# One over root of the norms' variances: ScalarE root and VectorE reciprocal, or a GpSimd power

## The chip, the cores and the metric

The kernel runs on one core of a Trainium2 chip. The metric is the device time of one execution in microseconds (us), as the median of several runs; lower is better. The core has five engines that run in parallel, each through its own instructions strictly in program order: TensorE (PE in the profile, PEld for its weight loads), VectorE (DVE), ScalarE (ACT), GpSimd (POOL) and SyncE (SP, which here only issues DMAs). They wait for one another by semaphores.

## The reference

Four layers work on an image batch x of shape (4, 56, 56, 128), each as `x = x + layer(_gn(x))`. Layers 0 and 3 are a window attention followed by a full attention over all 3136 pixels and an MLP, layer 1 is a selective scan in four directions, layer 2 is a deformable convolution. What this change concerns is the norms in them, all of which have one over the root of a variance:

```python
def _gn(v, G=32, eps=1e-5):
    g = v.reshape(B_, H_, W_, G, C_ // G)
    m = jnp.mean(g, axis=(1, 2, 4), keepdims=True)
    s = jnp.var(g, axis=(1, 2, 4), keepdims=True)
    return ((g - m) / jnp.sqrt(s + eps)).reshape(v.shape)

# layers 0 and 3, twice each (before the full attention, before the MLP)
def _layernorm(x, g, b, eps=1e-05):
    m = jnp.mean(x, axis=-1, keepdims=True)
    v = jnp.mean((x - m) ** 2, axis=-1, keepdims=True)
    return (x - m) * jax.lax.rsqrt(v + eps) * g + b

# layer 1, at its end
y = (y - mu) * jax.lax.rsqrt(var + LN_EPS) * ln_w + ln_b
```

## The kernel before

The four images are done one after the other, and per image the four layers. x lies in SBUF as 128 channels (partitions) by 3136 pixels, and most loops run over 7 chunks of 448 pixels. All phases below are written with a manual schedule: the order of the calls in the source is the order of the instructions on every engine, and nothing is reordered afterwards.

**Where the change sits.** Two helpers hold it. `group_norm` (line 117) is called 4 times per image, 16 in all: once at the head of each layer. It multiplies statistics by a small matrix on PE into PSUM (`gn_pv`, line 130), takes a root on ACT (line 132) and a reciprocal on DVE (line 133), for a 128x1 tile `gn_rstd`. `ln_spread` (line 150) is called once per chunk of every layer norm: 7 times in each of the 8 window phases, 7 in each of the 8 MLPs and 7 in each of the 4 ends of layer 1, 140 in all. Its PE products (`ln_pv`, line 156) give 448 variances as 112x4; ACT takes the root (line 158), DVE the reciprocal (line 159) into `ln_rs`. Later in program order `ln_rows` (line 167) or `scale` of `mamba_out` (line 1173) spreads `ln_rs` over all partitions again by PE (`ln_pb`).

**Window phase** (lines 376 to 470; windows at 219 to 302). A loop over u runs a pipeline of eight bands of windows together with the layer norm of chunk u-2. For one u the calls are, in this order: `scores(u)`, `out(u-1)`, `some` (four products `pm` on PE and their maxima `mx` on DVE, lines 349 and 350), `tokens(u+2)` (line 222, on POOL), `exponentials(u)` (line 267, ACT), `center(u-2)` (line 147 on PE, 383 on ACT), `normalize(u)` (sum and reciprocal on DVE, lines 271 and 272, then two products `pz` on POOL, line 275), `project(u+1)`, `spread(u-2)` (the helper above), `queries(u+1)`, `values(u+1)`, `some`, `scale(u-2)` (`ln_rows`: PE line 167, a copy on ACT line 168, a product on DVE line 392), `keys(u+1)` (four instructions on ACT, line 241), `some`, `turn(u)` (PE, line 281), `shift(u-2)` (ACT, line 395, writes `oTi`), `turned(u)` (ACT, line 286), `inputs(u-2)` (PE, lines 400 and 406), `some`, `weigh(u)`. Chunk 0 to 6 of the norm thus meets u = 2 to 8, and the band loop ends at u = 7.

At the head of that phase, `attention` clears `ks` and `qs` on POOL (lines 323, 324), then `group_norm` is called, then POOL clears `kl` (377), `xw0` (219), `qp0`, `kb0`, `pz0` (225), `xw1`, `qp1`, `kb1`, `pz1`. The first two bands' tokens are made on DVE (line 222, from x, `gn_mean` and `gn_rstd`); the first DVE instruction of them needs the clearing of `xw0`, which it overwrites.

**MLP** (lines 643 to 710). One chunk ahead: center, two of the four hidden products with GELU on ACT (680), spread, the other two, residual, `ln_rows`, result. **End of layer 1** (`mamba_out`, lines 1139 to 1195): per chunk c spread(c); mean(c+1) (PE 1149, DVE 1153, ACT 1155); gate(c+1) (DVE 137, PE 1163, ACT SiLU 1164); out(c-1) (PE 1184, DVE 1185); scale(c) (PE 1173, DVE 1175, ACT 1177, DVE 1178). POOL has nothing in this loop.

ScalarE's functions need a table: an instruction ACT_TABLE_LOAD stands in ACT's stream wherever the next function is not in the table loaded last. Roots, exponentials (267, 549, 819, 1002), GELU (680), SiLU (791, 1164) and logarithms (827) are of different tables here; copies, squares and identities (with scale and bias) cause none.

Of the kernel before, what the change touches and what calls it, by code (L numbers as in the profile page):

```python
# [10 lines left out]
F32 = mybir.dt.float32  # L11
F32R = mybir.dt.float32r
I32 = mybir.dt.int32
AF = mybir.ActivationFunctionType
ALU = mybir.AluOpType
# [4 lines left out]
P = 128  # L20
# [14 lines left out]
NKB = (L + KB - 1) // KB  # L35
QB = 112
NTB = L // QB
LP = NKB * KB
MW = 512
KW = L // MW * MW  # L40
# [14 lines left out]
def _swin_cols():  # L55
    return [("wq", 128), ("wk", 128), ("wv", 128), ("wo", 128),
            ("w1", 512), ("w2", 512), ("b1", 4), ("bq", 1), ("bk", 1),
            ("bv", 1), ("bo", 1), ("b2", 1), ("g1", 1), ("be1", 1), ("g2", 1), ("be2", 1)]


COLS = {
    "C": [("ident", 128), ("gmat", 128), ("center1", 128), ("center2", 128), ("others2", 128), ("ones1", 1), ("ones2", 1), ("lo", 1), ("dmask", TB), ("halves", HW), ("base", 2 * KK * NTB)],
    "L0": _swin_cols(),
# [7 lines left out]
def _offsets(cols):  # L71
    at, n = {}, 0
    for name, w in cols:
        at[name] = (n, w)
        n += w
    return at, n


class _Net:
    def __init__(self, ctx, tc, x, packs, out):  # L80
        self.tc, self.nc, self.x_in, self.out = tc, tc.nc, x, out
        self.B = x.shape[0]
        nc = self.nc
        wp = ctx.enter_context(tc.tile_pool(name="weights", bufs=1))
        self.keep = wp
        self.w = {}
        for i, (layer, cols) in enumerate(COLS.items()):
            at, n = _offsets(cols)
            t = wp.tile([P, n], F32, tag=f"w_{layer}", name=f"w_{layer}")
            (nc.sync if i % 2 == 0 else nc.scalar).dma_start(t, packs[layer])  # L90
            self.w[layer] = {name: t[:, o : o + k] for name, (o, k) in at.items()}
        c = self.w["C"]
        self.ident, self.gmat = c["ident"], c["gmat"]
        self.ones = {1: c["ones1"], 2: c["ones2"]}
        self.center = {1: (c["center1"],), 2: (c["center2"], c["others2"])}
        self.sel = wp.tile([P, KB], F32R, tag="sel", name="sel")
        nc.vector.memset(self.sel.bitcast(F32), 0.0)
        for h in range(NH):
            nc.vector.memset(self.sel[h * DK : h * DK + 2, :].bitcast(F32), 1.0)
        self.ident2 = wp.tile([64 + NX, NX], F32R, tag="ident2", name="ident2")  # L100
        nc.vector.memset(self.ident2.bitcast(F32), 0.0)
        for k in (0, 64):
            nc.vector.tensor_copy(self.ident2[k : k + NX, :], self.ident[:NX, :NX])
        self.one32 = wp.tile([P, DK], F32, tag="one32", name="one32")
        nc.vector.memset(self.one32, 1.0)
        self.eps = wp.tile([P, 1], F32, tag="eps", name="eps")
        nc.vector.memset(self.eps, 1e-5)
        self.x = wp.tile([P, L], F32, tag="x", name="x")
        self.st = wp.tile([P, NCK, 6], F32, tag="gn_st", name="gn_st")
        self.dpool = ctx.enter_context(tc.tile_pool(name="tables", bufs=1, space=DRAM))  # L110
# [6 lines left out]
    def group_norm(self, sb, ps):  # L117
        nc = self.nc
        st = self.st
        mv = sb.tile([P, 2], F32, tag="gn_mv", name="gn_mv")  # L120
        nc.vector.bn_aggr(mv, st.rearrange("p c s -> p (c s)"))
        pm = ps.tile([P, 512], F32, tag="mm", name="gn_pm")
        nc.tensor.matmul(pm[:, 0:1], lhsT=self.gmat, rhs=mv[:, 0:1], start=True, stop=True)
        mean = sb.tile([P, 1], F32, tag="gn_mean", name="gn_mean")
        nc.vector.tensor_copy(mean, pm[:, 0:1])
        dv = sb.tile([P, 1], F32, tag="gn_dv", name="gn_dv")
        nc.vector.tensor_sub(dv, mv[:, 0:1], mean)
        nc.vector.scalar_tensor_tensor(dv, dv, dv, mv[:, 1:2], ALU.mult, ALU.add)
        pv = ps.tile([P, 512], F32, tag="mm", name="gn_pv")
        nc.tensor.matmul(pv[:, 0:1], lhsT=self.gmat, rhs=dv, start=True, stop=True)  # L130
        rstd = sb.tile([P, 1], F32, tag="gn_rstd", name="gn_rstd")
        nc.scalar.activation(rstd, pv[:, 0:1], AF.Sqrt, bias=self.eps)
        nc.vector.reciprocal(rstd, rstd)
        return mean, rstd

    def gn_apply(self, out, x, gn):
# [13 lines left out]
    def ln_spread(self, sq, bank, sb):  # L150

        nc, n, k = self.nc, sq.shape[1], sq.shape[2] // QB
        pv = bank("ln_pv")
        for i in range(k):
            for j in range(n):
                nc.tensor.matmul(pv[:QB, i : i + 1], lhsT=sq[:, j, i * QB : (i + 1) * QB], rhs=self.ones[n][:, 0:1], start=(j == 0), stop=(j == n - 1))
        rs = sb.tile([QB, k], F32, tag="ln_rs", name="ln_rs")
        nc.scalar.activation(rs, pv[:QB, :k], AF.Sqrt, bias=self.eps[:QB])
        nc.vector.reciprocal(rs, rs)
        return rs  # L160

    def ln_rows(self, dst, rs, bank):
# [144 lines left out]
    def attention(self, layer, x, x1, oT, sb):  # L307
# [9 lines left out]
        nc, tc, w = self.nc, self.tc, self.w[layer]  # L317
        ks = sb.tile([P, LP], F32, tag="ks", name="ks")
        qs = sb.tile([P, LP], F32, tag="qs", name="qs")
        nm = sb.tile([P, L], F32R, tag="nm", name="nm")  # L320
# [892 lines left out]
    def deform(self, b, x):  # L1213
# [4 lines left out]
        tab = self.tables[b]  # L1218
        n2 = NTB * KK
        nq = CH // QB  # L1220
        with tc.tile_pool(name="df", bufs=1) as s1, tc.tile_pool(name="df_ps", bufs=1, space=PSUM) as s1x, tc.manual_schedule():
            idx = s1.tile([QB, n2], I32, tag="idx", name="idx")
            wps = s1x.tile([P, 2, 512], F32, tag="wt", name="wt")
            nw = 4 * KK * NTB // 2
            wts = [wps[:QB, i, :nw].rearrange("q (n k) -> q n k", k=4) for i in range(2)]
            with tc.tile_pool(name="dc", bufs=1) as sb, tc.tile_pool(name="dc_ps", bufs=6, space=PSUM) as ps:
# [4 lines left out]
                xg = sb.tile([P, L], F32, tag="xg", name="xgd")  # L1231
                gt = sb.tile([QB, NTB, P], F32, tag="gt", name="gt")
                tv = tab.rearrange("(t r x) (k c) -> r x t k c", r=2, x=TR, k=4)
# [68 lines left out]
            with tc.tile_pool(name="dg", bufs=2) as sb, tc.tile_pool(name="dg_ps", bufs=2, space=PSUM) as ps:  # L1302
# [10 lines left out]
                def weigh(t):  # L1313
                    g = patch[t].rearrange("q k (s c) -> q (k s) c", s=4)
                    wv = wts[2 * t // NTB][:, t % (NTB // 2) * KK : (t % (NTB // 2) + 1) * KK, :].rearrange("q k s -> q (k s)")
                    for k in range(0, 4 * KK, 12):
# [22 lines left out]

                for t in range(NTB + 1):  # L1340
                    if t < NTB:
# [117 lines left out]
```

## Time and profile before

| | |
|---|---|
| median of 14 runs | 13500.58 us (13492.34 to 13531.18) |
| the profiled execution: its own time | 13510.05 us |
| the profiled execution: span from first to last instruction | 13508.0 us |
| granted TensorE clock, mean | 0.936 |
| busy: DVE, ACT, POOL | 9225.0, 7563.5, 9948.9 us |
| ACT roots: lines 158 and 132 | 140 of 264 ns, 16 of 262 ns |
| DVE reciprocals: lines 159 and 133 | 140 of 178 ns, 16 of 164 ns |
| ACT_TABLE_LOAD, all lines | 365 of 1283 ns |
| a window phase (last image, layer 3) | 12642 to 12812 us |
| an end of layer 1 (last image) | 12136 to 12223 us |
| an MLP (last image, layer 3) | 13429 to 13505 us |

Times inside the span are given as us from its start. A line of the timeline reads: start, duration, engine, source line, operation, output<-inputs, shapes, count, and in brackets how long the engine was idle before it and what ended that idle time. In the chain of waits (the work that ended last, followed back) a line is start, duration, engine, tile, source line. In the groups it is the line, engine, operation, tiles, shapes and count, then busy us and mean ns.

### The profile page before, as it was taken

The numbers are of one execution on the slowest core, as the hardware profiler recorded it, in microseconds if no ns is written. First come the engines' busy times: TensorE is split into PE (matmuls) and PEld (weight loads), VectorE is DVE, ScalarE is ACT, GpSimd is POOL, SyncE is SP. The second block draws the span as 40 slices with busy tenths as digits, with TensorE's granted clock in tenths as the row PEclk, the third lists the DMA queues.
The fourth block names the chain that finished last, engine by engine and source line by source line (L and its number), as shares of the span: only waits on it lengthen the run. The fifth ranks groups of instructions, "written<-read, shape, count | busy, mean of one in ns | idle before, by whom it ended". The sixth has DMA issues, their size and how long they took to land.

```text
span 13508.0 us, 221295 instructions
## 1 busy us (share of the span) xinstructions
PE 11968.5 (89%) x87732; PEld 7700.9 (57%) x87732; DVE 9225.0 (68%) x11159; ACT 7563.5 (56%) x19130; POOL 9948.9 (74%) x6852
## 2 busy tenths in 40 slices
PE   8989995799998999579999899957999989995799
PEld 4448883544544888454454488845445448883544
DVE  6649993464665999446466599945646659993564
ACT  5567761356556776135655677613565567761356
POOL 4949994487494999448759499943975949994397
PEclk9999997899999999789999999978999999997899
DMA  2000004200000000420000000042000000004200
GB/s 98 1 13 5 4 4 123 68 1 8 4 1 13 5 4 4 127 64 1 8 4 1 13 5 5 3 129 63 1 11 1 1 13 5 5 3 132 60 1 6
DMA packets 181186, 344.79 MB, mean 26 GB/s; under 512 B 20104, under 2 KB 101416, under 8 KB 180024
## 3 DMA queue, kind: packets, MB, share of 16 engines
q0 software_dynamic: 80640, 231.28, 6.1%
q1 hardware_dynamic: 99224, 97.83, 2.3%
q8 instruction: 693, 11.35, 0.4%
q14 instruction: 341, 2.79, 0.1%
q10 hardware_dynamic: 288, 1.53, 0.0%
HBM read 256.04 MB, written 74.52 MB: 24 GB/s over the span
## 4 chain that ended last, share of the span: by engine, by line
PE 32%; DVE 9%; issue 3%; POOL 3%; ACT 3%; DMA 0%; SPq 0%; another core or an unknown queue 0%; DVEq 0%; POOLq 0%; ACTq 0%
PE pm L349 7%; DVE hs L1066 6%; PE po L571 4%; PE pst L547 3%; PE pst L542 2%; PE yt L1084 2%; PE dbu L1048 2%; PE pvt L1328 2%; POOL hs L1075 1%; PE pyb L1100 1%; DVE mx L350 1%; POOL g L1308 1%; DVE dgb L952 1%; PE pd L560 1%; PE pss L257 1%
## 5 line engine op out<-in xcount | busy, mean ns | idle before, releaser
L555 POOL TENSOR_TENSOR es<-es,e 128x896 f32<-128x896 f32 x2016 | 4160.9, 2090 | 131.4 <-ACT e L549 73.5
L350 DVE TENSOR_REDUCE mx<-pm 128x1 f32<-128x512 f32 (+1 forms) x4928 | 3058.2, 671 | 1413.3 <-PE pm L349 797.4
L549 ACT ACTIVATE e<-pst 128x448 f32<-128x448 f32 (+1 forms) x5600 | 2678.4, 544 | 1897.4 <-PE pst L547 1349.4
L1066 DVE TENSOR_TENSOR_SCAN hs<-da,dbu 128x928 f32<-128x928 f32 x1792 | 3632.9, 2070 | 54.5 <-ACT dbu L1059 30.3
L1075 POOL TENSOR_TENSOR hs<-hs,cb 128x896 f32<-128x896 f32 x1792 | 3464.0, 1944 | 25.5 <-ACT carry L1070 19.5
L349 PE MATMUL pm<-ks,qs 32*128 32x512 f32 (+1 forms) x9856 | 2917.2, 637 | 13.4 <-DVE nm L371 7.8
L547 PE MATMUL pst<-qs,ks 32*128 32x448 f32 x11200 | 2688.7, 548 | 0.0
L1084 PE MATMUL yt<-w_C,hs 128*116 128x128 f32 x14336 | 1866.0, 273 | 1.2 <-POOL hs L1075 1.2
L542 PE MATMUL pst<-nm,sel 32*128 32x448 f32 x5600 | 1640.0, 615 | 0.0
L1084 PEld LDWEIGHTS yt<-w_C,hs 128*116 128x116 f32 x14336 | 1571.0, 135 | 2.2 <-POOL hs L1075 2.1
L1048 PE MATMUL dbu<-dgb,ut 112*128 112x224 f32 x7168 | 1258.6, 298 | 269.1 <-DVE hs L1066 269.0
L1308 POOL DMA_INDIRECT g<-tab,idx x1008 | 943.5, 936 | 629.8 <-issue 435.5
L571 PE MATMUL po<-e,va 128*32 128x448 f32 (+1 forms) x11200 | 1352.4, 551 | 0.1
L349 PEld LDWEIGHTS pm<-ks,qs 32*128 32x128 f32 x9856 | 924.4, 186 | 746.4 <-DVE mx L350 621.1
L1328 PE MATMUL pvt<-w_C,g 112*128 112x112 f32 x4032 | 665.8, 324 | 701.9 <-issue 590.3
L1048 PEld LDWEIGHTS dbu<-dgb,ut 112*128 112x128 f32 x7168 | 945.3, 192 | 534.6 <-DVE hs L1066 524.5
L1002 ACT ACTIVATE da<-dl,A 128x112 f32<-128x112 f32 x3584 | 1194.5, 383 | 0.1
L547 PEld LDWEIGHTS pst<-qs,ks 32*128 32x128 f32 x11200 | 1099.8, 185 | 103.6 <-issue 14.7
L1328 PEld LDWEIGHTS pvt<-w_C,g 112*128 112x128 f32 x4032 | 561.1, 180 | 815.7 <-issue 792.2
L542 PEld LDWEIGHTS pst<-nm,sel 32*128 32x128 f32 x5600 | 570.6, 184 | 740.5 <-DVE mx L350 387.1
L1329 ACT COPY vt<-pvt 128x336 f32<-128x336 f32 x336 | 142.3, 441 | 1417.0 <-remote 972.3
L1070 ACT COPY carry<-hs 128x32 f32<-128x32 f32 x1792 | 398.1, 222 | 623.0 <-DVE hs L1066 614.9
(228 smaller groups left out, 15355.6 us busy)
## 6 DMA issues: line engine op xcount, KB each, us to landing
tab<-zero SPq DMA_DIRECT2D x4, 6728.0 KB
g<-tab,idx POOLq DMA_INDIRECT x1008
tab<-gt SPq DMA_DIRECT2D x32, 448.0 KB
dl_d<-dl SPq DMA_DIRECT2D x28, 448.0 KB
dl<-dl_d SPq DMA_DIRECT2D x56, 224.0 KB
tab<-gt SPq DMA_DIRECT2D x32, 336.0 KB
out_dram<-x SPq DMA_DIRECT2D x28, 224.0 KB
x<-in_x_dram SPq DMA_DIRECT2D x21, 224.0 KB
```

Of the source, the lines that this page charges most:

```text
L349: nc.tensor.matmul(pm[:, :m], lhsT=qs[head(h), q.start : q.start + P], rhs=ks[head(h), keys], start=True, stop=True)
L350: nc.vector.tensor_reduce(mx[:, home[i][1], h, kc : kc + 1], pm[:, :m], AX.X, ALU.max)
L542: nc.tensor.matmul(t[:, :CH], lhsT=self.sel[head(h), :], rhs=nm[head(h), part(qc)], start=True, stop=False)
L547: nc.tensor.matmul(t[:, :CH], lhsT=ks[head(h), k * KB : (k + 1) * KB], rhs=qs[head(h), part(qc)], start=False, stop=True)
L549: nc.scalar.activation(e[:nk, j, :], t[:nk, :CH], AF.Exp, scale=SCALE)
L555: nc.gpsimd.tensor_tensor(s, es[g - 1, p][:nk] if k == 1 else s, e[:nk], ALU.add)
L571: nc.tensor.matmul(m["po"][head(h), :CH], lhsT=va[:nk, k, head(h)], rhs=src(h)[:nk], start=(k == 0), stop=(k == NKB - 1))
L1048: nc.tensor.matmul(pu[:, 8 * h : 8 * h + 8, 2 + tb * TB : 2 + (tb + 1) * TB], lhsT=made[g]["ut", 2 * r + tb][:, d, :], rhs=made["r", g // ...
L1066: nc.vector.tensor_tensor_scan(flat(pairs[u // 2][:, d % 2]), flat(made[g]["da"][:, r]), flat(banks.pop(u)), 0.0, ALU.mult, ALU.add)
L1075: nc.gpsimd.tensor_tensor(hs, hs, made["r", g // 2]["cb"][:, :, r * HW : (r + 1) * HW], ALU.mult)
L1084: nc.tensor.matmul(sums[q][:YR, e * P : (e + 1) * P], lhsT=hs[:, n, :], rhs=self.ident, start=(n == 0), stop=(n == NST // 2 - 1), is_trans ...
L1328: nc.tensor.matmul(pt[:, m, :], lhsT=g[:, k + m, s * P : (s + 1) * P], rhs=self.ident[:QB, :QB], start=(s == 0), stop=(s == 3), is_transpo ...
```

## The change

The root on ACT becomes an addition of epsilon on DVE (PSUM to SBUF), and the reciprocal on DVE becomes a power of -0.5 on POOL, in place, with a constant tile of exponents as second operand. The constant tile `eps` goes, `half` (128x4) comes.

```diff
+EPS = 1e-5
+NQ = 4
...
-        self.eps = wp.tile([P, 1], F32, tag="eps", name="eps")
-        nc.vector.memset(self.eps, 1e-5)
+        self.half = wp.tile([P, NQ], F32, tag="half", name="half")
+        nc.vector.memset(self.half, -0.5)
...
         rstd = sb.tile([P, 1], F32, tag="gn_rstd", name="gn_rstd")
-        nc.scalar.activation(rstd, pv[:, 0:1], AF.Sqrt, bias=self.eps)
-        nc.vector.reciprocal(rstd, rstd)
+        nc.vector.tensor_scalar_add(rstd, pv[:, 0:1], EPS)
+        nc.gpsimd.tensor_tensor(rstd, rstd, self.half[:, 0:1], ALU.pow)
...
         rs = sb.tile([QB, k], F32, tag="ln_rs", name="ln_rs")
-        nc.scalar.activation(rs, pv[:QB, :k], AF.Sqrt, bias=self.eps[:QB])
-        nc.vector.reciprocal(rs, rs)
+        nc.vector.tensor_scalar_add(rs, pv[:QB, :k], EPS)
+        nc.gpsimd.tensor_tensor(rs, rs, self.half[:QB, :k], ALU.pow)
```

## The prediction

> **What bounds the kernel now.** I read the page's busy times first, then the table loads by source line, then the timeline and the chain of waits of each stage that calls the two helpers.
>
> ```profile
> PE 11968.5 (89%) x87732; PEld 7700.9 (57%) x87732; DVE 9225.0 (68%) x11159; ACT 7563.5 (56%) x19130; POOL 9948.9 (74%) x6852
> ```
>
> Over the span PE is busiest and ACT least, so work taken from ACT pays only where ACT's turn comes last. The change can act in the stages with norms alone: 8 window phases (about 165 us each), 8 MLPs (76), 4 ends of layer 1 (87) and 16 group norms.
>
> ```profile
> L158 ACT ACT_TABLE_LOAD  x132: 1283/1283/1283, 62.0 to 13491.8; - x132
> ```
>
> The root's own price on ACT is small (264 ns); the table loads are what it costs: 132 here, 8 at line 132, and those that bring the other table back. Without roots one load per phase stays: at line 267, 48 become 8, at 680, 56 become 8, at 1164, 28 become 4, at 549, 8 become none. That takes away 132+8+40+48+24+8 = 260 loads, 334 us of ACT, and 41 us of roots. How little of it is on the path, one window iteration (u = 4, layer 3, last image) shows in the timeline:
>
> ```profile
> 12724.10 1.28 ACT L267 ACT_TABLE_LOAD   x1
> 12724.13 2.22 DVE L350 TENSOR_REDUCE mx<-pm 128x1 f32<-128x448 f32 x4 [0.44 <-PE pm L349]
> ...
> 12725.40 0.86 ACT L267 ACTIVATE s<-s 128x784 f32<-128x784 f32 x1
> ...
> 12726.28 0.97 DVE L271 TENSOR_REDUCE m<-s 128x16 f32<-128x784 f32 x1
> 12726.70 1.28 ACT L158 ACT_TABLE_LOAD   x1
> ...
> 12726.74 0.95 PE L156 MATMUL ln_pv<-w_C,ln_sq 128*112 128x1 f32 x8 [0.26 <-ACT ln_sq L383]
> ...
> 12727.69 3.08 POOL L275 TENSOR_TENSOR pz<-s,m 64x784 f32<-64x784 f32 x2 [13.81 <-DVE m L272]
> ...
> 12728.29 0.18 DVE L159 RECIPROCAL ln_rs<-ln_rs 112x4 f32<-112x4 f32 x1 [0.75 <-ACT ln_rs L158]
> ...
> 12729.58 1.14 PE L167 MATMUL ln_pb<-w_C,ln_rs 112*128 112x112 f32 x8
> ...
> 12730.75 0.53 ACT L168 COPY ln_sq<-ln_pb 128x448 f32<-128x448 f32 x1 [1.86 <-PE ln_pb L167]
> ...
> 12731.18 2.37 ACT L241 ACTIVATE kb<-pk,w_L 32x392 f32<-32x392 f32 x4
> ...
> 12733.58 0.76 ACT L395 ACTIVATE oTi<-ln_sq,w_L 128x448 f32<-128x448 f32 x1
> ```
>
> PE waited only 0.26 us for all that both loads and the root delay. The root's result was there at 12728.5, a microsecond before PE got to `ln_pb` at 12729.58. From `ln_pb` on, the chain runs through ACT: copy, four `kb`, `oTi`, and then PE's line 400.
>
> **The price of the power, p.** No row shows a power on POOL. The nearest are its elementwise products:
>
> ```profile
> L994 POOL TENSOR_TENSOR du<-dl,xa 128x112 f32<-128x112 f32 x896 | 408.3, 457 | 1.8 <-DMA dl<-dl_d 1.5
> L1011 POOL TENSOR_TENSOR dh<-du,dh 128x448 fp32r<-128x448 f32 x224 | 255.6, 1141 | 30.4 <-ACT dh L1007 30.4
> ```
>
> From 112 to 448 elements costs 684 ns, 2.0 ns each, so a product of 4 elements would be an estimated 0.24 us. A power has more steps. Lower end 0.15 us (POOL's clearing of 128x64 takes 152 ns), upper end 0.94 us, its dearest non-streaming row (an indirect DMA, 936 ns); I take 0.5, near the 112-element product. A software routine several times dearer is kept as a rival. The addition on DVE I put at 0.16 us, as other 128x1 operations there (line 125), plus 0.05 a hand-over.
>
> **Window phases, the term that decides.** `spread(u-2)` comes after `normalize(u)` in program order, so on POOL the power stands behind the two `pz` (12727.69 to 12730.77), although its input is ready at about 12727.9. Neither starts earlier: `pz` needs lines 271 and 272 on DVE, these stand behind the four `mx`, which end at 12726.35 and come from PE. The earlier exponential (12724.1 instead of 12725.4) therefore frees nothing here; in u = 5, where line 271 had waited 0.39 us for it, it does. So `ln_rs` is ready at 12730.77 + 0.1 + p, and `ln_pb` begins 1.29+p late. The same subtraction gives 1.28 in u = 2, 0.9 in u = 5 and 1.4 in u = 7; I take 1.2+p. Behind `ln_pb` wait PE's next `pm` and `turn`, and on ACT the copy, `kb` and `oTi`, with no gap to absorb it (0.5 us before `oTi` is all, and that follows `kb`). In u = 8 no `pz` stands ahead: nothing. 8 phases x 6 x (1.2+p) = 57.6+48p = **+82 us**.
>
> **Heads of the window phases.** POOL's clearings from `kl` on stood ahead of nothing and ran early; now they queue behind the power, which waits for the statistics. First, DVE's line 222 needs `xw0`: power, `kl` and `xw0` instead of root and reciprocal, +0.54+p (in the three later layer-0 heads less 1.28, a load exposed there). Second, line 222 then meets seven clearings on POOL (8.1 us). What that does, two layer-3 heads show, where one clearing string still ran:
>
> ```profile
> 12645.45 5.63 DVE L222 TENSOR_SCALAR xw<-x,gn_mean,gn_rstd 128x343 f32<-128x343 f32 x3
> ```
>
> ```profile
> 2532.95 1.46 DVE L222 TENSOR_SCALAR xw<-x,gn_mean,gn_rstd 128x343 f32<-128x343 f32 x3
> ```
>
> Undisturbed the three take 0.89 us. In images 0 and 2 DVE got in after one clearing, in 1 and 3 only after the whole string (5236 ns for one instruction). Block per head from 0.7 to 8 us; I take 4.3, half and half. Sum: 8(0.54+p+4.3), less 3x1.28, less the 10.6 us that layer 3's heads lose already: 24+8p = **+28**.
>
> The Trainium skill ("SBUF — State Buffer", Who interferes with whom) has the pair of ports that DVE and GpSimd share held for a whole instruction, with the other engine blocked. The 5.24 us agrees that DVE is shut out, but it lasted over four clearings (1.81 at most), where the rule has it wait for one; by the rule the block would be about 1.8 at most and the sum 20 us lower.
>
> **Other group norms.** Layer 1: the load at line 132 (882.00 to 883.28) and root and reciprocal lay on the path, 1.78 us; now 0.25+p: 4(p-1.53). Layer 2: about 4(p-0.25). Together 8p-7 = **-3**.
>
> **MLPs.** From the second chunk the chain of waits is PE alone, period 9.21 us; root and loads hide behind it. The variance is there at 13454.97, `ln_pb` comes at 13457.17, so the power has some 1.9 us of cover behind one POOL addition long done (13453.99). Uncovered are the first chunk, p-0.24, and 0.2 us that PE waits at 13493.64: 8(p-0.44) = **+0.5**. The GELU's loads leave no gap in PE.
>
> **Ends of layer 1.** Chain of waits:
>
> ```profile
> 12163.85 1.41 ACT xc L1177 x2
> 12165.26 0.02 issue
> 12165.28 1.28 ACT L158
> 12166.58 0.27 ACT ln_rs L158
> 12166.85 0.02 issue
> 12166.87 0.18 DVE ln_rs L159
> 12167.05 1.04 DVE xc L1153 x2
> ```
>
> Here the load is on the path: DVE's reciprocal holds up line 1153 behind it. But next late is DVE itself: line 1178 runs 12165.30 to 12166.39, then the addition, so 1153 starts at about 12166.6 instead of 12167.05. Five chunks x 4 x 0.42 = **-8**. POOL is idle and `ln_pb` comes 8 us later: the power is covered. ACT's SiLU loads lie before a product that PE delivers later. The attention's first load (line 549) is in no chain.
>
> The skill ("ScalarE: Activation LUTs", What ACT_TABLE_LOAD costs) adds 1380 ns of drain to each 1283 ns load. This trace has the root start 0.02 us after its load ended (12727.98, 12728.00). With the drain, layer 1's group norms would gain 5.5 us more.
>
> **Sum:** 57.6+24-7-3.5-8 = 63, and 72p (48+8+8+8): at p = 0.5, +99 us, on the profiled execution's own 13510.05 (span 13508.0). That execution lay 9.5 us above the median of the runs; I carry the difference over to the median, 13500.6+99 = **13600 us**, +0.7%.
>
> **Rivals.**
> 1. *The power is a slow routine.* Nothing in the trace excludes it. Above p = 1.9 the MLPs become bound by it too (8 x 6 chunks, 48 us for each us more): p = 2 gives +212 (13713), p = 4 about +450 (13950).
> 2. *Not slower: the power does not wait for `pz`*, because `pz` gets done, or the power issued, before PE reaches `ln_pb`. The place is POOL's queue in u = 2 to 7, the point from which it decides is `ln_rs` ready by 12729.5. For it: POOL idles 13.8 us ahead of `pz`. Against: the program order, and `mx` ahead of line 271. Then a window phase gains PE's small gaps, 0.26 to 0.8 us in five iterations, 8 x 1.8 = -14, and with the other terms (24-7-3.5-8+24p = +18) the change is +4, or -25 where the heads get in at the first clearing: 13476 to 13535.
> 3. *The loads stay* because other functions still alternate. The ACT list shows only one table besides the root's in each of these phases, so hardly; it would cost +115 or so (no gains in layer 1): 13615.
>
> **Numbers.** Forecast 66%; slow power 18%; not held up 12%; loads stay 4%. The forecast's own range is p 0.15 to 0.94 and heads 0.7 to 8 us: 63+11-29 = +45 to 63+68+30 = +161. For 8 in 10 I reach on to part of rivals 1 and 2: +34 to +220, 13535 to 13720. What a measurement of this kernel can tell from no change is about 0.2%, 27 us. Slower by more: 66+18+4, less 3 = 0.85; within: 0.10; faster: 0.05.
>
> **What would show it.** On POOL's timeline, the power right after the second `pz` in u = 2 to 7 and its duration p; PE idle before `ln_pb`, ended by POOL; window iterations of about 21 us instead of 19.2 to 19.8; heads where line 222 lasts as long as the clearings; 105 table loads left; layer-1 iterations 0.4 us shorter. It is wrong if the power takes several us, or if `ln_pb` isn't late.

## The result and the profile after

The changed kernel takes 13694.01 us (median of 6 runs, 13687.82 to 13702.53) against 13500.58 (28 runs now, 13483.56 to 13531.18): a ratio of 1.0142, 95% interval 1.0132 to 1.0152, **slower by 193 us**. Its profiled execution took 13690.59 us, span 13688.8, granted clock 0.930. The spans of the two profiled executions differ by 180.8 us; the rest lies in where each stood to its median (9.5 above, 3.4 below). In `kernel.py` of the changed kernel, lines behind the two new constants have moved by 2: 158 is 160 (DVE's addition) and 161 (the power), 167 is 169, 222 is 224.

The page's busy times, to set beside the line of before:

```profile
PE 11997.7 (88%) x87732; PEld 7739.2 (57%) x87732; DVE 9267.0 (68%) x11159; ACT 7210.1 (53%) x18713; POOL 10100.3 (74%) x7008
```

ACT lost 353 us (104 table loads are left of 365), POOL gained 151 us (156 powers), and the kernel became slower: neither engine's total was the bound. The powers, in the groups by shape (the figures behind the bar are busy us and mean ns of one, then the idle time ahead and what ended most of it):

```profile
L161 POOL TENSOR_TENSOR ln_rs<-ln_rs,half 112x4 f32<-112x4 f32 x140 | 142.3, 1016 | 508.2 <-DVE ln_rs L160 504.4
L135 POOL TENSOR_TENSOR gn_rstd<-gn_rstd,half 128x1 f32<-128x1 f32 x16 | 9.0, 564 | 71.0 <-DVE gn_rstd L134 71.0
```

So p is 1.02 us for four elements per partition and 0.56 for one. The window iteration that the prediction showed (u = 4, layer 3, last image), in the timeline of after:

```profile
12903.67 0.10 DVE L160 TENSOR_SCALAR ln_rs<-ln_pv 112x4 f32<-112x4 f32 x1
12903.91 3.07 POOL L277 TENSOR_TENSOR pz<-s,m 64x784 f32<-64x784 f32 x2 [16.18 <-DVE ln_rs L160]
12904.35 1.03 PE L351 MATMUL pm<-ks,qs 32*128 32x448 f32 x8
...
12907.06 1.02 POOL L161 TENSOR_TENSOR ln_rs<-ln_rs,half 112x4 f32<-112x4 f32 x1
...
12908.14 1.72 PE L169 MATMUL ln_pb<-w_C,ln_rs 112*128 112x112 f32 x8 [2.76 <-POOL ln_rs L161]
```

The power's input is ready at 12903.77, but POOL starts it 3.3 us later, behind `pz`. PE ends `pm` and stands still for 2.76 us, released by the power; before, the line `ln_pb` had no wait. From the iteration's start (the last `pwy`) to `ln_pb` it is 9.56 us, before 7.25. The eight `ln_pb` products then take 1.72 us; before they took 1.14. At the head of the same phase the chain of waits shows:

```profile
12809.45 0.58 POOL gn_rstd L135
12810.03 0.27 POOL kl L379
12810.30 0.47 POOL xw L221
12810.77 0.03 issue
12810.80 8.62 DVE xw L224 x3
```

Here 8.62 us stand for three DVE instructions that take 0.89 undisturbed, and all eight heads have 8.60. The timeline has DVE's three and POOL's string beside them, the first and the last of the seven clearings shown:

```profile
12810.71 0.73 POOL L227 MEMSET qp<- 128x768 f32 x1
12810.80 8.61 DVE L224 TENSOR_SCALAR xw<-x,gn_mean,gn_rstd 128x343 f32<-128x343 f32 x3 [1.43 <-POOL xw L221]
...
12816.98 1.79 POOL L227 MEMSET pz<- 128x2048 f32 x1
```

Where the 180.8 us lie, from the two traces by stage, all four images together (us, after less before): window phases +191.3, attentions +9.4, MLPs -3.0, heads of layer 1 and its convolution -6.5, scans -1.8, ends of layer 1 -10.3, layer 2 +1.7. Inside the eight window phases: from the group norm to DVE's line 224 +3.9, its first three instructions +51.1 (17.7 to 68.8), from there to the first `pwy` (PE's product of the output weights, one per u, line 299 before) -2.5, the seven iterations from `pwy` to `pwy` +157.8 (997.1 to 1155.0), from the last `pwy` to the attention's first exponential -19.1.

### The profile page after: what moved, and what is told of

Read it like the earlier page. It is cut to its first block, busy times and chain, and to the rows that moved or that the text cites. A ratio compares the mean times of both kernels' runs of the same rounds, so it can differ in the third digit from the quotient of the medians.

```text
span 13688.8 us, 221078 instructions
## 1 busy us (share of the span) xinstructions
PE 11997.7 (88%) x87732; PEld 7739.2 (57%) x87732; DVE 9267.0 (68%) x11159; ACT 7210.1 (53%) x18713; POOL 10100.3 (74%) x7008
## 5 line engine op out<-in xcount | busy, mean ns | idle before, releaser
L277 POOL TENSOR_TENSOR pz<-s,m 64x784 f32<-64x784 f32 x128 | 192.0, 1500 | 832.4 <-DVE ln_rs L160 514.7
```

## The experiments

The theory: (a) in the iterations, POOL's order puts the power behind `pz`; (b) in the heads, the clearings that now run behind the power shut DVE out; (c) TensorE's clock falls to half after the new wait, which the forecast had left out. The rivals are that the power's own price does it all, and that the change acts elsewhere. These runs fell on several chips. On most of them, as `before_again` shows below, the stage of the deformable gathers takes 1312 us instead of 1529, with the other stages alike; so ratios to the kernel before on the same chip are compared, and iterations and heads, which a gather doesn't touch.

**pow_first** issues the power ahead of the products `pz` on POOL:

```diff
 def normalize(t):  # sum and reciprocal on DVE
-    for j in range(2): nc.gpsimd.tensor_tensor(pz...)
+def products(t):
+    for j in range(2): nc.gpsimd.tensor_tensor(pz...)
...
 do("spread", u - 2)
+if u != 1: do("products", u)
```

> The changed kernel, but in the window phases POOL gets the power of spread(u-2) ahead of the two pz products of normalize(u); PE, DVE and ACT keep their order. Theory (the power is late because it stands behind pz on POOL): ln_rs is then ready before PE reaches ln_pb, the window iterations u = 3 to 7 fall from 21.5 to 23.9 us back to 19.2 to 19.9, the seven iterations of all eight phases together from 1155 to about 990 us, and the time from 13694 to about 13530. Rival (the power's own duration of 1.0 us, with the hand-overs DVE to POOL to PE, is what delays): the iterations keep 1 us or more of the loss, time above 13600. Rival (pz itself becomes late, and turn(u) on PE waits for it): PE idle before the pt products instead of before ln_pb, iterations near 21 us.

Measured: 13331.92 us, ratio 1.0049 (1.0032 to 1.0066). The iterations sum to 987.9 us, 9 less than in before; the heads stay at 8.6 us each. In the timeline (u = 5, layer 3, last image):

```profile
12566.76 1.03 POOL L161 TENSOR_TENSOR ln_rs<-ln_rs,half 112x4 f32<-112x4 f32 x1 [12.01 <-DVE ln_rs L160]
...
12567.77 3.07 POOL L281 TENSOR_TENSOR pz<-s,m 64x784 f32<-64x784 f32 x2
...
12568.11 1.14 PE L169 MATMUL ln_pb<-w_C,ln_rs 112*128 112x112 f32 x8
```

The power of the same 1.03 us is done at 12567.79, PE reaches `ln_pb` 0.3 us later without a wait. So the order, not the power's price alone, made the 158 us: (a) holds. The time fell less than expected (about 13530 would be a ratio of 1.0022), and one reason is in the trace: from the last `pwy` to the attention's first exponential it takes 255.5 us again, as in before (254.3), where after has 235.3.

**clear_first** puts the clearings of `kl`, `xw`, `qp`, `kb`, `pz` ahead of the group norm; the power stays behind `pz` (`gn()` is the call of `group_norm`):

```diff
+for t in range(2):
+    for z in (xw, qp, kb, pz): nc.gpsimd.memset(z[t], 0.0)
+gn = gn()
...
-    if t < 2:
-        nc.gpsimd.memset(xw[t], 0.0)
...
-    if t < 2:
-        for z in (qp, kb, pz):
-            nc.gpsimd.memset(z[t], 0.0)
```

> The changed kernel, but kl, xw, qp, kb and pz are cleared on POOL ahead of the group norm's power instead of behind it. Theory (DVE's first token instruction is shut out while the clearings run): the three DVE instructions of line 222 of the kernel before fall from 8.60 us in all eight heads to 0.9 in the layer-0 heads and to 1.5 to 5.7 in the layer-3 heads, as before the change; together with the shorter wait for xw this takes 45 to 55 us off: about 13645. The window iterations stay at 21.5 to 23.9 us. Rival (what delays line 222 is the power or the DVE addition ahead of it, not the clearings): no change, 13694.

Measured: 13437.9 us, ratio 1.0127 (1.0110 to 1.0144), where 13645 would be 1.0107. From the answer on the tile `xw` (ns minimum, median, maximum, then first and last start):

```profile
L226 DVE TENSOR_SCALAR xw<-x,gn_mean,gn_rstd x48: 283/383/509, 23.2 to 12567.9; 128x343 f32<-128x343 f32 x16, 128x28 f32<-128x28 f32 x16, 128x21 f32<-128x21 f32 x16
```

No instruction of the line is over 0.51 us (before 5.24, after 8.21): the three take 0.88 us in every head, so (b) holds. But part of the gain is paid back: in layer 3 the string of clearings (12552.3 to 12561.1 in the last image) is still running when the statistics are there, the power starts at 12561.08 behind it, and from group norm to line 226 it takes 8.17 us in three of the four and 8.40 in the last, instead of 3.56. Heads together 54.3 us against 98.9 in after, iterations unchanged (1167).

**both** has the two edits together.

> pow_first and clear_first in one. Theory (two independent queue effects on POOL carry the loss): the gains add, 13694 - 165 - 50 = about 13480, which is 20 us below the kernel before, from the ends of layer 1 (-10), the group norm of layer 1 (-6) and the last part of the window phases. Rival (the power costs in other places as well): it stays above 13510.

Measured: 13295.21 us (10 runs), ratio 1.0017 (1.0007 to 1.0026); iterations 991.8, heads 53.7. The two losses go away together, but the 20 us below before did not come: the rival's 13510 is a ratio of 1.0007, and the measured one lies above it. Its trace has the attentions 14.1 us longer than `before_again` has, of which more below. `best` and `early` ask what can be won.

**gn_root** gives root and reciprocal (and the constant `eps`) back to the group norms alone, **ln_root** to the row norms alone; the lines are those of gn_root, in ln_root they stand the same for `rs`:

```diff
-nc.vector.tensor_scalar_add(rstd, pv[:, 0:1], EPS)
-nc.gpsimd.tensor_tensor(rstd, rstd, self.half[:, 0:1], ALU.pow)
+nc.scalar.activation(rstd, pv[:, 0:1], AF.Sqrt, bias=self.eps)
+nc.vector.reciprocal(rstd, rstd)
```

> Half of the change: the 16 group norms have root and reciprocal again, the 140 layer norms keep the addition and the power. Theory: the heads of the window phases go back to those before (head and line 222 together minus 55 us), layer 1's group norm gets its table load back (+6), the window iterations stay: about 13645. Rival (heads cost little and the loss is all in the iterations): 13690 or more.

> The complement of gn_root: root and reciprocal for the row norms as in the kernel before, the power on GpSimd for the group norms alone. Theory: the window iterations are those of before (997 us, within 10), all that is lost stays in the heads, where DVE's line 222 is shut out by the clearings as in after (about 8.6 us per head, +50 to +55 us against before), and the group norms of layers 1 and 2 give 5 to 20 us back: ratio 1.002 to 1.004. Rival (heads and iterations act on each other, or the heads' loss is made up within the phase): ratio 1.000 or below, or iterations that differ from before by over 20 us.

Measured: gn_root 13428.33 us, ratio 1.0120 (1.0103 to 1.0137), iterations 1147.4, heads 35.9 (before 43.9). ln_root 13317.69, ratio 1.0039 (1.0023 to 1.0054), iterations 998.9, heads 99.1. Each has one loss whole and the other not at all. The excesses, 1.20% and 0.39%, add up to 1.59%, within the intervals of the 1.48% that the change costs on such a chip (`after_again`).

**mult** (the row norms' power becomes a product in the same place) and **fill** (two matmuls ahead of `ln_pb`) ask how the 157.8 us divide:

```diff
-nc.gpsimd.tensor_tensor(rs, rs, self.half[:QB, :k], ALU.pow)      # mult
+nc.gpsimd.tensor_tensor(rs, rs, self.half[:QB, :k], ALU.mult)
...
 pb = bank("ln_pb")                                                # fill, u = 2 to 7
+for i in range(2):
+    nc.tensor.matmul(pb[:, :CH], lhsT=self.ident, rhs=self.x[:, :CH], start=True, stop=True)
```

> After's kernel with the power of the row norms replaced by a product on the same tiles: the root of the variance is left out, and the instruction stays in its place with its wait. The power's own price: 1.02 us in 112x4 against an estimated 0.24 us for a product of 4 elements. Theory (the power stands on the path in u = 2 to 7, behind pz): ln_pb begins 0.78 us earlier in 48 iterations, -37 us, and with a shorter wait of TensorE (about 1.5 to 2 us instead of 2.3 to 2.8) somewhat less time at half clock, up to -35 us more: iterations 1155 to 1085-1118, ratio 1.009 to 1.0115. pz's 1.2 to 1.3 us stay, so the iterations do not come back to the 997 of before. Rival (the power itself is cheap or hidden, only the order costs): iterations 1150 or more, ratio 1.014.

> After's kernel with two more matmuls of TensorE in each of the window iterations u = 2 to 7 (identity by a 448-column block of x, into the bank of ln_pb, which ln_pb then overwrites), placed ahead of ln_pb, so that TensorE works while it would wait for the power. They add 2.0 us of work per iteration where it waits 2.3 to 2.8. Theory (what the forecast missed in the window iterations, 158 us measured against 48 x (1.2+1.02) = 106, is TensorE's clock falling to half after that wait): TensorE's time at half clock in these iterations goes to nearly none (after: 0 to 10.2 us per iteration), and the seven iterations of the eight phases, 1155 us together, come down by 30 to 55 us, though TensorE has 98 us of work more; the whole about -30 to -60 us against after's 13694, a ratio of 1.010 to 1.012 to the kernel before. Rival (the missing 50 us are waiting of some other kind, and the half clock is only seen with it): the added work cannot help, 1155 us or up to 50 us more, ratio 1.014 or above.

Measured, mult: 13359.47 us, ratio 1.0073 (1.0058 to 1.0088), iterations 1094.7. The product takes 0.20 us:

```profile
L161 POOL TENSOR_TENSOR ln_rs<-ln_rs,half 112x4 f32<-112x4 f32 x140 | 28.1, 201 | 500.4 <-DVE ln_rs L160 496.7
```

Iterations are 60 us below after's, where 0.82 us less in 48 places make 39; the rest goes with the clock (116.0 us of them at half, in after 245.8). The ratio is below the range expected, above all because the MLPs fell too, by 37 us together, which the expectation hadn't priced; TensorE ran 14 us at half clock there, against 94 in after. How the shorter instruction brings that about was not traced.

Measured, fill: 13440.52 us, ratio 1.0131 (1.0116 to 1.0147), iterations 1126.6, 28 to 37 less than in the two traces of the changed kernel though TensorE does more. The ratio misses the range of 1.010 to 1.012, and its interval overlaps that of `after_again`; what shows the effect is the iterations. The window of the iteration u = 4 (last phase), first in after, then in fill (from:to and length, busy us of PE, PEld, DVE, ACT, POOL, then the granted clock):

```profile
12898.00:12920.00 22.00, 19.21 (x140) 12.88 (x139) 13.95 (x27) 9.95 (x20) 6.50 (x6) 0.92 0.00 1
```

```profile
12652.00:12674.00 22.00, 20.11 (x147) 13.16 (x145) 14.34 (x28) 9.92 (x20) 6.50 (x6) 1.00 0.00 1
```

And `ln_pb` in fill, u = 4:

```profile
12658.92 1.77 PE L169 MATMUL ln_pb<-x,w_C 128*128 128x448 f32 x4
...
12661.75 1.15 PE L171 MATMUL ln_pb<-w_C,ln_rs 112*128 112x112 f32 x8 [1.06 <-POOL ln_rs L161]
```

It still waits for the power, but the products behind are back at 1.15 us. TensorE's time at half clock in the 56 iterations: 245.8 us in after, 64.9 in fill, 37.5 in before. With the clock whole the iterations read off the waits themselves:

| iteration, us | u = 4 to 5 | 5 to 6 | 6 to 7 |
|---|---|---|---|
| before | 19.17 | 19.84 | 19.17 |
| mult, typical, clock whole | 20.66 | 20.88 | 20.67 |
| fill, clock whole | 21.48 | 21.71 | 21.48 |
| after, mean of eight | 22.13 | 22.83 | 22.81 |

From before to fill is 2.31, 1.87, 2.31: the forecast's 1.2 + p with p = 1.02. From mult to fill is 0.82: the two prices on POOL, 1.016 less 0.201. From fill to after is 0.65 to 1.33: the clock. After itself confirms it: in the two of its eight phases that have no half clock from u = 4 to 5, that iteration takes 21.49 us, fill's time without fill's matmuls. (c) holds in the iterations, a little below the 30 to 55 us that were expected, since fill keeps 65 us of half clock, most of it behind u = 7. Over u = 2 to 7, fill with the clock whole (20.89, 21.75, 21.48, 21.71, 21.48, 19.78 us) is 14.5 us above before with the clock whole (18.30, 19.45, 19.17, 19.84, 19.17, 16.70): 116 us in eight phases are wait, the other 42 of the 157.8 the clock.

**best** is pow_first with the root kept in the window phases' group norms; **early** is best with `ln_pv` ahead of `pk` on PE and the addition ahead of DVE's sums; **early_root** has early's order with the roots of before. The order of early, against after:

```diff
 do("center", u - 2)
-if u != 1: do("normalize", u)
-do("project", u + 1)
+do("project", u + 1, "q")
 do("spread", u - 2)
+if u != 1: do("normalize", u)
 if u != 1: do("products", u)
+do("project", u + 1, "k")
```

> Both power orders mended in the cheapest way found: in the window phases the power of a row norm goes to GpSimd ahead of the two products pz, and the group norm at the heads of the window phases keeps the root on ScalarE and the reciprocal on DVE; the power stays for the group norms of layers 1 and 2 and for all row norms. From pow_first's ratio of 1.0049 (65 us) less the heads' +55: about +5 us, between -15 and +20, ratio 0.999 to 1.0015; iterations about 990 us, heads (to the end of the first three DVE instructions) about 44 as before, layers 1 and 2 -15 to -25. Rival (the stages' sums decide: iterations -9, heads 0 to -8, layers 1 and 2 -20, nothing lost elsewhere): -30 us, ratio 0.998 or below.

> best, with the row norm's variance taken one place earlier on TensorE (ln_pv ahead of the projection pk instead of behind it) and its addition ahead of DVE's line of sums for pz. In best the power ends at 1.0 us after the point where pz could have begun, so in u = 2 and 3, where no attention group lies between, TensorE waits 1.5 to 1.9 us for pz, and the next stretch often runs 3.41 us at half clock. Theory (the power's 1.0 us ahead of pz is what keeps best at the time of before): power and pz begin about 0.5 to 0.7 us earlier, the waits in u = 2 and 3 fall to about 1 us, iterations 994 to 960-980 us: ratio 0.998 to 0.9995. Rival (the path there runs through ACT's copy, kb and oTi, and pz's wait is hidden behind it): iterations 985 or more, ratio 1.000 to 1.001 as for best.

> The kernel before, with root and reciprocal everywhere, and only the order of early: ln_pv ahead of pk on TensorE, the variance's chain ahead of DVE's line of sums. Theory (early's gain over before needs the loads gone): before's ln_pv already waits 0.26 to 0.80 us for ln_sq, which stands behind the exponential's table load on ACT; without pk ahead of it it waits up to 0.66 us longer, so nothing is gained: iterations 993 to 1020, ratio 0.9995 to 1.002. Rival (early's gain is the order's alone and the power has no part in it): iterations 985 or less, ratio 0.9985 or below.

Measured, best: 13277.91 us (11 runs), ratio 1.0004 (0.9995 to 1.0013): the time of before, not below it. Iterations 994.3. In u = 4 to 6 they are 18.65, 18.78 and 18.65 us, 0.5 to 1.1 below before, but in u = 2 and 3 the power delays `pz` and PE waits for it; one stretch of 3.41 us at half clock then lengthens an iteration from 18.92 to 20.12 us. By stage against `before_again`, layer 1 is 21.3 us shorter, while attentions and MLPs are 24.3 longer, with 118 us at half clock in the MLPs instead of 86.

Measured, early: 13245.51 us (9 runs), ratio **0.9974** (0.9965 to 0.9984), 32 us below before and the one version faster than both kernels. The ratio is below the ranges of both theory and rival, and the mechanism expected was little of it: iterations 990.7, not 960 to 980. Of the 48 us between the traces of best and early, 27 are in the ends of the window phases, 261.9 to 235.1 us together, and 17.5 in the MLPs. For the ends the clock shows why. The windows below begin at the last `pwy` of the last phase, in best, then in early:

```profile
12572.00:12587.00 15.00, 14.10 (x48) 6.93 (x49) 7.43 (x14) 3.36 (x7) 1.01 (x1) 0.54 0.01 2
```

```profile
12530.00:12549.00 19.00, 16.68 (x93) 8.79 (x93) 13.34 (x26) 5.50 (x14) 1.01 (x1) 1.00 0.00 1
```

Ahead of that `pwy` PE waited 0.93 us for `pz` and then 1.84 for `o` (DVE's copy, line 307) in best, 1.15 and 1.84 in early, and behind it PE's order is the same. Yet in best the clock is at half for 13.65 us soon after, in early not at all; the ends hold 184.6 us of half clock in best and 86.6 in early. In each trace all stretches at half clock start on a grid with steps of 3.413 us. In best the wait of 1.84 us lies within one step and is 54% of it; in early an edge of the grid cuts it, and its step is idle for 45%. In seven phases of best the last `pwy` stands at 0.61 to 0.65 of a step, with 21 to 25 us at half clock to follow in the end; in six of early it stands at 0.42 to 0.45, with 10. So what a wait costs depends on where it falls, and early's gain rests partly on that: against `before_again`, 23 us of its gain are these ends and 24 layer 1, and the attentions take 15 back.

Measured, early_root: 13526.24 us (9 runs; 13489.02 before on its chip), ratio 1.0025 (1.0015 to 1.0035). Iterations 1050.3, 0.65 us more in each of u = 4 to 6 as expected, more in u = 2 and 3; both sum and ratio lie above the ranges expected (1020 and 1.002). `ln_pv` waits for the square, which stands behind the exponential and its table load (u = 5):

```profile
12789.85 0.95 PE L156 MATMUL ln_pv<-w_C,ln_sq 128*112 128x1 f32 x8 [1.46 <-ACT ln_sq L383]
```

The new order alone therefore costs time; it needs the loads gone.

**after_again** and **before_again** are the two kernels themselves on one of those chips.

> The changed kernel itself, beside the other runs on one chip. Both theories: about 193 us over before as on the first chip, ratio 1.0142 to 1.0147; window iterations 1155 within 15, first three DVE instructions of the heads 68.8.

> The kernel before itself, for a trace from the same chip as best and early. Window iterations 997, heads 44 us together, and the stage of the deformable gathers as short as in the other runs here (about 1311 instead of 1529 us), with nothing else changed.

Measured: after_again 13477.18 us, ratio 1.0148 (1.0133 to 1.0164), iterations 1163.8, first three DVE instructions 68.8. before_again 13275.03 us, iterations 992.8, heads 35.6 (the two heads that had 5.6 us are not among them here), gathers 1312.1.

## Why the prediction was right, and where its sizes were off

**Direction and place were right.** The power stands behind the two `pz` in u = 2 to 7, `ln_pb` begins 2.31 us late in u = 4 where 1.29 + 1.02 was the rule, POOL is what PE waits for, 104 table loads are left (105 forecast), and the ends of layer 1 are shorter (-10.3, and -6.0 by the second pair of traces; forecast -8). `pow_first` shows that the order does it.

**The price p** was put at 0.5 us and is 1.016 for the row norms: the term "8 phases x 6 x (1.2+p)" becomes 106 us instead of 82, +25. The nearest row chosen, the product of 112 elements, was no guide to a power; the upper end, 0.94, was just short. For a product the estimate by size (0.24 us for 4 elements) was good: mult has 0.20.

**The clock** is missing from that term. The iterations lost 157.8 us, not 106. Some 10 us of the rest are wait, most of it in u = 7: the forecast took its 1.4 + p from a phase in which before was itself at half clock there, and with the clock whole the iteration grows by 3.08 us. The other 42 are TensorE at half clock behind the wait. The Trainium skill ("TensorE: Matmul & The Clock Gate", Part 1) states that the clock drops to half after an idle window of about 3.4 us, and that the window runs freely. The stretches here agree in length (3.41 us and multiples of it) and in standing on a grid of such steps: the 180 of after start within 0.03 us of one place in steps of 3.413 us. They differ in one point: the step need not be idle throughout. In after, of the steps at full clock in which PE ran no matmul for 60% of the time or more, 91 of 100 were followed by half clock; between 35 and 60% it was 70 of 155, below that 18 of 3189. The 2.76 us of u = 4 are 81% of the step that ends at 12908.54, and the next one is at half clock. In `mult`, where that wait is 1.93 to 2.23 us in u = 4 to 6, 18 of the 24 iterations u = 4 to 6 have no half clock; in after, with 2.76 to 3.07 us, it is 3 of 24.

**The heads**, "Block per head from 0.7 to 8 us; I take 4.3, half and half", was the step that was read wrongly. It is not half and half: the three instructions take 8.60 us in all eight heads, +51.1 us in place of some 24 net of what before lost already. Once DVE is released by POOL's own clearing of `xw0`, POOL goes straight on with the next clearing, and DVE does not get in until the string ends. The forecast's upper bound, 8 us, was near the answer (7.71 more than the 0.89 undisturbed). With 24+8p = 28.5 at the measured 0.56, the heads came to +54.9.

The small terms: MLPs -3.0 (+0.5 forecast), heads of layers 1 and 2 about -6 (-3). **Not foreseen**: the ends of the window phases became 19 us shorter, with 134 us at half clock before and 91 after, and the attentions 9 us longer. In every kernel with the row norms' power the attentions are 9 to 15 us above the kernel before of their kind of chip, with more half clock (52 us in after, 37 in before); in `ln_root` and `early_root`, without it, they are not, and in `mult` by 2 us only. What sets this off was not tried.

**The rivals.** A slow routine was not it: p is below the 1.9 us at which the MLPs would be bound. The power was held up. The loads went. Put together: 106 for the iterations, about 52 more there (10 of wait, 42 of clock), 55 in the heads, -22 between heads and first `pwy` and at the phases' ends, -10 elsewhere, make 181. That is beyond the forecast's own range (+161 at p = 0.94 and 8 us per head), by the clock, and inside the wider one, which had been drawn for a dearer power: that the time fell inside it is, for the clock's part, luck. The single figure, +99, was about half of what came.

## What to carry to other kernels

When work moves to an idle engine, read that engine's queue at the moving instruction's place in program order: 14 us of idle time a step earlier did not help, because 3 us of other work stood ahead of it. An engine that gets a wait also holds up all that was queued behind it, here seven clearings that then ran against DVE. A new wait of a few us on TensorE should be priced with the half clock that may follow it; and the gain of an offload may need a second edit, of the order: pow_first took the loss in the iterations back by it, and early came out ahead of the kernel before, partly by where its waits fall on the clock's grid.

## What the hardware showed

- A power on POOL takes 564 ns for 128x1 and 1016 ns for 112x4, a product there 201 ns for 112x4.
- DVE, once POOL's string of clearings had started, was kept out over the whole string: 8.2 us for one instruction that takes at most 0.51 undisturbed. The Trainium skill ("SBUF — State Buffer", "Who interferes with whom") has the lock held for one instruction at a time; the longest clearing takes 1.81 us, so here the string counts and not the instruction.
- TensorE's half clock came in stretches on a fixed grid of 3.413 us, after a step of the grid that was largely idle: after 91 of 100 steps idle for 60% or more, after 18 of 3189 idle for less than 35% (trace of after). Of 323 steps at half clock that were idle for 20% or more, none was followed by full clock. A wait of 1.84 us was followed by 13.65 us at half clock where it fell into one step (54% of it), and by none where an edge cut it (45%). One stretch of 3.41 us at half clock lengthened an iteration by 1.2 us.
- The same kernel's gather stage took 1529 us on one chip and 1312 on others.
